# Cross-attention with layer norms: two more vectors loaded as columns, and the softmax's weights left unnormalised up to the last layer norm

## The chip, the cores and the metric

The kernel runs on one core of a Trainium2 chip. A core has a matrix engine (TensorE, PE in the profile, with its weight loads as PEld), a vector engine (VectorE, DVE), a scalar engine (ScalarE, ACT), a general engine (GpSimd, POOL) and a queue that issues transfers (SyncE, SP). Each works through its own list of instructions in order and waits on semaphores for the others. The metric is the time in microseconds on the device, from launch to end. A profile is one execution of the program, with a record for nearly each instruction.

## The reference, cut to what matters

```
text_p  = H_l @ W_text + b_text            # H_l: 4 x 2048 x 512
audio_p = H_a @ W_audio + b_audio          # H_a: 4 x 77 x 384
Q = layer_norm(text_p, g1, beta1);  K = layer_norm(audio_p, g2, beta2);  V = audio_p
alpha = softmax(Q @ K^T / sqrt(512))
H_hyper = (alpha @ V) @ W_out + b_out
out = layer_norm(H_hyper + H_l, g_out, beta_out)
layer_norm(x) = (x - mean) * rsqrt(var + 1e-5) * gamma + beta
```

All is in fp32. The last layer norm is what the change rests on. If a row z is multiplied by a positive number s, its mean and deviation are multiplied by s and its variance by s squared, so that with EPS times s squared in the place of EPS the normalised row is the same. Here s is the sum of the softmax's exponentials of that row.

## The kernel before

**Preparation** (to about 41 us). The keys' input (308 rows, in three blocks) is multiplied by W_audio, normalised (`statistics`, `normed`) and turned (`value_turned`, `key_turned`). W_text is centred and turned into wct (`turn_text`), and its Gram matrix is formed in four parts (`gram`, L633, bank names w_ps). The query is never formed: the score of a row x with a key is x times a matrix of "score weights" m_ps (`score_weights`, L328), 128 x 4 x 80 for each of four blocks of the 512 inputs. Of the 80 columns of each of the four sequences 77 are keys, one is for the bias b_text, and two are padding (S = 77, S1 = 80). They are written zero in kg, on VectorE (L312), and pass through the matmul. `score_offsets` (L346) gives what the biases and beta1 add to the scores, out of rowst, a 128 x 128 stationary operand for each block, whose first 64 columns hold centred b_text times g1, 64 times over, and the last 64 beta1.

To have these as columns, b_text and beta1 are each loaded 64 times over as rows (L158, L159: one tile `rows`, 64 partitions each), b_text is centred on VectorE (L690 to L692), and TensorE turns the tile in four transposes into rows_ps (L698), from which bcv (VectorE, L699) and rowst (ScalarE, L703, L704) are taken. The vectors g1, g2 and beta2 come in another way: as three small loads of 4 x 128 into vec_rows (L152), turned by one transpose (vec_ps, L678) into the columns vec (L679). bc2, the bias's sum of squares, is formed by ScalarE on 64 partitions (L709) and copied to the other 64 (L710).

**The loop** goes over 64 tiles of 128 rows. The tiles are grouped in batches for the small work: twelve of four tiles, then seven of two and two of one. One letter names each step of a tile n or of a batch (named after its first tile):

- p, P: projection of the tile on TensorE (L440 into y, L448 into yl); x: VectorE turns the input of a later tile (L391); t, s: VectorE sums for the norm of the query and adds to the scores (L464, L486)
- r: POOL's rsqrt for the query's norm (L494, L215); c: VectorE scales the scores and takes the maximum (L501, L504); e: ScalarE's exponentials, with their sum by an accumulator (L511)
- w, W: TensorE turns the weights, two tiles at a time (L523), and ScalarE copies them out (L524). The bank is that of yl for the next projection
- i: VectorE takes the reciprocal of the batch's sums, in place (L537)
- a: TensorE multiplies the weights with V @ W_out (L531, bank h); z: VectorE forms z = h * inv + x and its sum (L544)
- q: ScalarE's squares of z less its mean (L552); n: minus the mean (L558); d: variance plus EPS for a batch in one ScalarE instruction (L564), then POOL's rsqrt
- the normalisation is done in one of two ways: o and y on ScalarE (L592, L597) followed by m on POOL (times go, plus beo, L601 and L602), or v and V on VectorE (L581, L583). Each then stores the tile through SP (L571).

The order of the first 40 tiles is a loop over `run`; from then on it is a list written out by hand, for example `p44 v35 o32 r40 i36 y33 W36 V35 z37 a36`. `in_program_order` fixes each engine's list to this order. The planning of buffers (pools of a fixed number of tiles by tag) decides which waits are inserted.

Of the kernel before, what the change touches and what calls it, by code (L numbers as in the profile page):

```python
# [23 lines left out]
F32 = mybir.dt.float32  # L26
# [22 lines left out]
def tile_xattn(  # L49
# [34 lines left out]
    work = ctx.enter_context(tc.tile_pool(name="work", bufs=3))  # L84
    zs = ctx.enter_context(tc.tile_pool(name="zs", bufs=13))
    small = ctx.enter_context(tc.tile_pool(name="small", bufs=8))
    ps1 = ctx.enter_context(tc.tile_pool(name="ps1", bufs=1, space=bass.MemoryType.PSUM))
# [61 lines left out]

    vec_rows = const.tile([3 * NH, P], F32, name="vec_rows")  # L150
    for i, v in enumerate((g1, g2, beta2)):
        nc.sync.dma_start(  # L152
            out=vec_rows[i * NH : (i + 1) * NH, :], in_=v.rearrange("(j p) -> j p", p=P)
        )

    HP = P // 2
    rows = const.tile([P, H], F32, name="rows")
    nc.sync.dma_start(out=rows[:HP], in_=b_text.partition_broadcast(HP))  # L158
    nc.sync.dma_start(out=rows[HP:], in_=beta1.partition_broadcast(HP))  # L159

# [39 lines left out]
    nc.gpsimd.memset(mhalf, -0.5)  # L200
    eps = const.tile([P, 1], F32, name="eps")
    nc.gpsimd.memset(eps, EPS)
    warm = const.tile([P, T], F32, name="warm")
# [14 lines left out]
    rowst = const.tile([P, NH, P], F32, name="rowst")  # L218
    bcv = const.tile([P, NH, 1], F32, name="bcv")
    bc2 = const.tile([P, 1], F32, name="bc2")  # L220
    vec = const.tile([P, 3 * NH], F32, name="vec")
    mu = [const.tile([P, ND, Q, AQ], F32, name=f"mu_{i}") for i in range(2)]
# [87 lines left out]
    def keys_scaled():  # L310

        nc.vector.memset(kg[:, :, :, S:], 0.0)  # L312
        for b in range(B):
            nc.vector.tensor_copy(kg[:, :, b, S : S + 1], bcv)
        for j in range(NH):
            nc.vector.tensor_scalar(
                kg[:, j, :, :S],
                kt[:, j, :].rearrange("p (b s) -> p b s", s=S),
                vec[:, j : j + 1],
                None,  # L320
                ALU.mult,
            )

    def score_weights(k, tag):

        pm = flat(bank(tag, f"m_ps_{k}"))[:, : B * S1].rearrange("p (b s) -> p b s", s=S1)
        for j in range(NH):
            nc.tensor.matmul(  # L328
                pm,
                lhsT=wct[:, j, k * P : (k + 1) * P],  # L330
                rhs=kg[:, j],
                start=(j == 0),
                stop=(j == NH - 1),
            )
        for b in range(2):
            (nc.vector.tensor_copy if b else nc.scalar.copy)(
                mu[b][:, k, :, :SQ], parts(pm[:, b, :])
            )
        nc.scalar.copy(later[:, k], pm[:, 2:, :])
# [68 lines left out]
    class Batch:  # L408


        def __init__(self, tiles):
# [8 lines left out]
            self.ss, self.rs = map(columns, ("ss", "rs"))  # L420
            self.mx, self.inv = map(columns, ("mx", "inv"))
            self.sz, self.sq, self.ro, self.nm = map(columns, ("sz", "sq", "ro", "nm"))
            self.z = {}

# [81 lines left out]
    def exponential(f):  # L506
        s = state[f]
        for q in range(s.m):
            c = slice(q, q + 1)
            e = s.e[:, q, :S]  # L510
            nc.scalar.activation(e, e, AF.Exp, bias=s.mx[:, c], accum_out=s.inv[:, c])  # L511

    def turn_weights(f, a=0):
# [10 lines left out]
        nc.scalar.copy(s.et[:, a:z, :], pe[:S, a:z, :])  # L524

    def apply(n):

        s, c = of(n)
        s.h = getattr(s, "h", {})
        s.h[n] = flat(bank("h", f"h_{n}"))  # L530
        nc.tensor.matmul(  # L531
            s.h[n], lhsT=s.et[:, n - s.tiles[0], :], rhs=s.vw, start=True, stop=True
        )

    def invert(f):
        s = state[f]
        nc.vector.reciprocal(s.inv[:, : s.m], s.inv[:, : s.m])  # L537

    def residual(n):

        i, t = divmod(n, T)
        s, c = of(n)
        z = s.z[n] = zs.tile([P, H], F32, name=f"z_{n}", tag="z")
        nc.vector.scalar_tensor_tensor(  # L544
            z, s.h.pop(n), s.inv[:, c], xs[i][:, t, :], ALU.mult, ALU.add, accum_out=s.sz[:, c]
        )

    def squares(n):
# [11 lines left out]
    def deviations(f):  # L560

        s = state[f]
        m = s.m
        nc.scalar.activation(  # L564
            s.ro[:, :m], s.sq[:, :m], AF.Identity, bias=eps, scale=float(H) ** -3
        )
        rsqrt(s.ro[:, :m], s.ro[:, :m])
# [30 lines left out]

    def norm_on_gpsimd(n):
        z = of(n)[0].z[n]  # L600
        nc.gpsimd.tensor_tensor(z, z, go, ALU.mult)  # L601
        nc.gpsimd.tensor_tensor(z, z, beo, ALU.add)  # L602
        store(n)

# [72 lines left out]
    pt = bank("gain", "vec_ps")  # L677
    nc.tensor.transpose(pt[:, 0, : 3 * NH], vec_rows, ident[: 3 * NH, : 3 * NH])  # L678
    nc.vector.tensor_copy(vec, pt[:, 0, : 3 * NH])  # L679
    value(2, pv[2])  # L680
# [7 lines left out]
    bmean = const.tile([P, 1], F32, name="bmean")  # L688
    b = rows[:HP]
    nc.vector.tensor_reduce(bmean[:HP], b, AX.X, ALU.add)  # L690
    nc.vector.tensor_scalar_mul(bmean[:HP], bmean[:HP], 1.0 / H)
    nc.vector.tensor_scalar(b, b, bmean[:HP], None, ALU.subtract)  # L692
    normed(2)
    gram(1)
    value_turned(2, "prep")
    key_turned(2, "gain")

    pt = rows_turned(rows, P, "h", "rows_ps")  # L698
    nc.vector.tensor_scalar_mul(bcv, pt[:, :, 0:1], 2.0)  # L699
    gram(2)  # L700
    keys_scaled()
    for j in range(NH):
        nc.scalar.mul(rowst[:, j, :HP], pt[:, j, :HP], vec[:, j : j + 1])  # L703
    nc.scalar.mul(rowst[:, :, HP:], pt[:, :, HP:], scale)  # L704
    for k in range(ND - 1):
        gram_out(k)
    gram(3)
    junk = scrap.tile([P, H], F32, name="sqj_b", tag="sqj")
    nc.scalar.activation(junk[:HP], b, AF.Square, accum_out=bc2[:HP])  # L709
    nc.vector.tensor_copy(bc2[HP:], bc2[:HP])  # L710
    gram_out(3)
    turn(0)
    turn(1)
    for k, tag in reversed(list(enumerate(("prep", "h", "gain", "h")))):
        score_weights(k, tag)
    score_offsets()
# [28 lines left out]
    def keep_warm_late(count):  # L745
# [16 lines left out]
        W=lambda f: turn_weights(f, T // 2),  # L762
        i=invert,
        a=apply,
        z=residual,
        q=squares,
        n=minus_mean,
        d=deviations,
        o=norm_shift,
        y=norm_on_scalar,  # L770
        m=norm_on_gpsimd,
        v=lambda n: norm_on_vector(n, 0),
# [12 lines left out]
    for n in range(40):  # L785
# [5 lines left out]
        if t == 0:  # L791
            run([("r", 4)], n)
        run([("v", 12), ("V", 12)] if on_vector else [("m", 12)], n)
        if n == KEPT:
# [13 lines left out]
    for step in """  # L808
        s39 z33
        p40 r36 o28 P40 x42 t40 y30 a35 z35 s40 a34 c36 y31 z34 x43  # L810
        p41 y28 P41 m30 t41 n32 s41
        p42 m31 P42 t42 m28 x44 q34 s42 e36 w36
        p43 q33 x45 q35 P43 t43 a37 d32 s43
        p44 v35 o32 r40 i36 y33 W36 V35 z37 a36 y34 y29 c40 q37 m33 P44 z36 m29 y32 a38 t44 z38 q36 x46 e40
        p45 s44 m34 q38 a39 P45
        p46 P46 z39 t45 n36 q39 s45 t46 d36 x47 x48 w40 i40 s46
        p47 a41 o36 y38 v37 t47 x49 W40 z41 a40 y36 y39 V37 z40 P47 s47 a42 a43
        p48 m32 m38 P48 q41 z42 q40
        p49 q42 r44 x50 z43 q43 t48 n40 c44 m36 d40 s48 v41 e44 w44 P49 a45 t49 o40 x51 V41 m39 y43 a44 W44 i44
        s49 z44 r48 z45  # L820
        p50 t50 y42 q44 a47 x52 c48 q45 z47 P50 e48 a46 q47 m43 s50 z46 v40 m42 q46
        p51 w48 n44 P51 t51 d44 V40
        p52 i48 s51 v47 a49 o44 a48 x54 x53 r50 y46 P52 y45 m46 y44 V47 c50 t52 z48
        p53 e50 z49 q48 w50 q49 P53 s52 m44 a51 t53 n48 d48 a50 s53 i50
        p54 o48 y48 r52 x55 P54 z50 z51 m45 t54
        p55 c52 P55 s54 n50 q51 q50 d50 m48 x57 e52 x56 w52 o50
        p56 t55 x58 s55 P56 y51 v49 r54 i52 t56 V49 a53 x59 c54 a52
        p57 y50 e54 z52 z53 m51 w54 P57 i54 s56 a54 a55 m50 t57
        p58 q53 x60 s57 q52 n52 z55 d52 r56 z54 P58
        p59 o52 t58 y52 c56 q55 s58 v53 e56 i56 q54 w56 P59 n54 a57 m52 d54 t59 o54 V53 y54 y55 s59 a56 z57 r58  # L830
        z56 q56 q57 m54
        p60 c58 x61 t60 P60 x62 n56 d56 e58
        p61 s60 w58 v56 i58 t61 V56 P61 o56 a59 s61 y57 a58
        p62 x63 P62 m55 r60 m57 z59 z58 t62 q59
        p63 n58 c60 q58 d58 s62 v58 t63 e60 r62 w60 i60 V58 c62 o58 P63 s63 a60 e62 w62 r63 z60 i62 y59 a61 q60
        z61 a62 n60 c63 q61 z62 e63 d60 k7 w63 k2 n62 a63 v60 i63 v61 V60 z63 q62 m59 V61 d62 v62 n63 v63 q63 V62 d63
        V63
    """.split():
# [37 lines left out]
```

## Time and profile before

| | us |
|---|---|
| median of 3 runs | 294.62 (294.55 to 294.77) |
| the profiled execution's own time | 294.76 |
| its span, first to last instruction | 293.0 |
| PE busy | 283.7 (97%) |
| DVE busy | 227.1 (78%) |
| ACT busy | 154.5 (53%) |
| POOL busy | 157.6 (54%) |

In the profile a row of a timeline is: start in us, length in us, engine, line, operation, output and inputs with their shapes, how many such instructions were merged, and in brackets how long the engine had been idle before and what ended that. The chain of work that ended last is followed back from the last instruction to what released each step. L numbers are lines of the kernel before. An fp32 matmul has two records in the profile, one for each pass. A row of small DVE instructions may overlap the next, so the distance from start to start is what it takes from the queue.

### The profile page before, as it was taken

What the parts mean: (1) busy time and instruction counts of PE and PEld (TensorE: products, weight loads), DVE (VectorE), ACT (ScalarE), POOL (GpSimd) and SP (SyncE); (2) the same over time, 40 slices, a digit from 0 to 9 for tenths busy, and PEclk for the clock granted to TensorE, in tenths of its full rate; (3) what the DMA queues carried; (4) which work ended last, traced back from release to release, by engine and by line L of the source; (5) the groups of instructions that cost most, each with busy time, mean ns of one, the idle gap of its engine ahead of it and who ended that gap; (6) DMA issues with size and microseconds to landing.
All of it is one profiled execution on the core that took longest, in us unless ns stands there. A gap on an engine that the chain in (4) does not pass through costs nothing.

```text
span 293.0 us, 3988 instructions
## 1 busy us (share of the span) xinstructions
PE 283.7 (97%) x1021; PEld 168.1 (57%) x1021; DVE 227.1 (78%) x713; ACT 154.5 (53%) x490; POOL 157.6 (54%) x168
## 2 busy tenths in 40 slices
PE   7999999999999999999999999999999999999990
PEld 5485755565555555555555565656565555555540
DVE  0784143486878797979797979798999999989996
ACT  3574210041446383737373737357967767477572
POOL 1012000010116667666666676677988978977834
PEclk9999999999999999999999999999999999999996
DMA  7999904358391876878787878789789996712214
GB/s 200 269 306 339 232 12 88 69 175 195 135 242 39 168 261 151 280 160 274 154 277 154 276 159 274 159 272 192 275 172 294 205 258 189 177 72 84 109 62 179
DMA packets 54315, 55.59 MB, mean 190 GB/s; under 512 B 2618, under 2 KB 35706, under 8 KB 54292
## 3 DMA queue, kind: packets, MB, share of 16 engines
q1 hardware_dynamic: 54291, 55.33, 69.9%
q8 instruction: 8, 0.13, 0.2%
q14 instruction: 16, 0.12, 0.1%
HBM read 38.23 MB, written 16.78 MB: 188 GB/s over the span
## 4 chain that ended last, share of the span: by engine, by line
PE 92%; DVE 3%; DMA 2%; issue 1%; SPq 1%; DVEq 0%; ACT 0%
PE y L440 53%; PE h L531 18%; PE yl L448 5%; PE vw_ps L370 4%; PE m_ps L328 3%; PE et_ps L523 2%; PE va_ps L266 2%; PE w_ps_yl L633 2%; DMA wa<-in_L_xattn_W_audio_dram 2%; PE w_ps_y L633 1%; DVE z L583 1%; PE uw_ps L346 1%; DVE z L544 1%; DVE y L581 1%; PE kt_ps L248 0%
## 5 line engine op out<-in xcount | busy, mean ns | idle before, releaser
L440 PE MATMUL y<-mu,xt 128*128 128x464 f32 (+2 forms) x512 | 179.6, 473 | 0.0
L440 PEld LDWEIGHTS y<-mu,xt 128*128 128x128 f32 x512 | 89.7, 190 | 49.6 <-issue 32.3
L531 PE MATMUL h<-vw,et 77*128 77x512 f32 x128 | 64.1, 594 | 0.1
L552 ACT ACTIVATE sqj<-z,sz 128x512 f32<-128x512 f32 x64 | 46.0, 719 | 31.9 <-DVE z L544 30.9
L601 POOL TENSOR_TENSOR z<-z,go 128x512 f32<-128x512 f32 x44 | 56.0, 1272 | 9.9 <-ACT z L597 9.4
L602 POOL TENSOR_TENSOR z<-z,beo 128x512 f32<-128x512 f32 x44 | 55.9, 1271 | 3.4
L544 DVE SCALAR_TENSOR_TENSOR z<-h,inv,x 128x512 f32<-128x512 f32 x64 | 46.4, 732 | 2.3 <-PE h L531 1.7
L391 DVE STREAM_TRANSPOSE xt<-xq 128x512 f32<-128x512 f32 x64 | 44.7, 703 | 0.5 <-PE y L440 0.5
L464 DVE CUSTOM_DVE_ANT_1 yl<-yl,x,bc 128x128 f32<-128x128 f32 x64 | 22.6, 353 | 28.2 <-PE yl L448 28.1
L464 DVE CUSTOM_DVE_ANT_1 y<-y,x,e 128x384 f32<-128x384 f32 x64 | 40.1, 626 | 2.3
L494 POOL TENSOR_SCALAR rs<-ss 128x4 f32<-128x4 f32 (+2 forms) x21 | 4.7, 225 | 67.7 <-DVE ss L464 67.6
L448 PEld LDWEIGHTS yl<-ub,xt 128*128 128x128 f32 x128 | 23.6, 188 | 26.2 <-issue 15.6
L597 ACT ACTIVATE z<-z,no,ro 128x512 f32<-128x512 f32 x44 | 34.5, 802 | 0.1
L524 ACT COPY et<-et_ps 77x256 f32<-77x256 f32 (+1 forms) x33 | 11.9, 362 | 39.4 <-PE et_ps L523 39.4
L215 POOL TENSOR_TENSOR ro<-ro,mhalf 128x4 f32<-128x4 f32 (+2 forms) x21 | 18.2, 869 | 23.8 <-ACT ro L564 23.7
L511 ACT ACTIVATE e<-e,mx 128x77 f32<-128x77 f32 x64 | 22.2, 350 | 11.9 <-DVE mx L504 11.9
L531 PEld LDWEIGHTS h<-vw,et 77*128 77x128 f32 x128 | 23.3, 190 | 7.0 <-issue 5.2
L448 PE MATMUL yl<-ub,xt 128*128 128x128 f32 x128 | 24.5, 273 | 0.0
L215 POOL TENSOR_TENSOR rs<-rs,mhalf 128x4 f32<-128x4 f32 (+2 forms) x21 | 18.6, 887 | 1.7
L486 DVE TENSOR_TENSOR e<-y,uws 128x80 f32<-128x80 f32 x64 | 14.9, 233 | 4.7 <-PE y L440 3.4
L523 PEld LDWEIGHTS et_ps<-ident,e 128*77 128x77 f32 x64 | 9.4, 147 | 15.1 <-issue 10.9
L581 DVE SCALAR_TENSOR_TENSOR y<-z,nm,gain_ps 128x512 f32<-128x512 f32 x20 | 14.9, 751 | 0.8
(112 smaller groups left out, 253.5 us busy)
## 6 DMA issues: line engine op xcount, KB each, us to landing
xq<-in_x_dram SPq DMA_DIRECT2D x64, 256.0 KB, 4.9
x<-in_x_dram SPq DMA_DIRECT2D x16, 1024.0 KB, 6.7
out_dram<-z SPq DMA_DIRECT2D x64, 256.0 KB, 2.3
wc<-in_L_xattn_W_text_dram SPq DMA_DIRECT2D x4, 256.0 KB, 5.7
wo<-in_L_xattn_W_out_dram SPq DMA_DIRECT2D x1, 1024.0 KB
wa<-in_L_xattn_W_audio_dram SPq DMA_DIRECT2D x3, 256.0 KB, 3.6
ba<-in_L_xattn_b_audio_dram SPq DMA_DIRECT2D x1, 256.0 KB, 5.6
bo<-in_L_xattn_b_out_dram SPq DMA_DIRECT2D x1, 256.0 KB
```

The lines of the kernel that those rows point to most:

```text
L215: nc.gpsimd.tensor_tensor(dst, v, mhalf[: v.shape[0], : v.shape[1]], ALU.pow)
L391: nc.vector.transpose(xt.rearrange("p k (a j) -> p a k j", j=R), xq[i][:, t].rearrange("p a (k i) -> p a k i", i=R),)
L440: nc.tensor.matmul(parts(y[:, : Q * AQ])[:, :, cols], lhsT=xt[:, k, :], rhs=mub[:, k, :, cols], start=(k == LAST_K), stop=(k == 0),)
L448: nc.tensor.matmul(b, lhsT=xt[:, k, :], rhs=ub.rearrange("p q i -> p (q i)"), start=True, stop=True)
L464: nc.vector.tensor_tensor_reduce(out=y, in0=y, in1=x, scale=1.0, scalar=first, op0=ALU.mult, op1=ALU.add, accum_out=to)
L511: nc.scalar.activation(e, e, AF.Exp, bias=s.mx[:, c], accum_out=s.inv[:, c])
L531: nc.tensor.matmul(s.h[n], lhsT=s.et[:, n - s.tiles[0], :], rhs=s.vw, start=True, stop=True)
L544: nc.vector.scalar_tensor_tensor(z, s.h.pop(n), s.inv[:, c], xs[i][:, t, :], ALU.mult, ALU.add, accum_out=s.sz[:, c])
L552: nc.scalar.activation(junk, s.z[n], AF.Square, bias=s.sz[:, c], scale=-float(H), accum_out=s.sq[:, c])
L597: nc.scalar.activation(z, z, AF.Identity, bias=s.no[:, c], scale=s.ro[:, c])
L601: nc.gpsimd.tensor_tensor(z, z, go, ALU.mult)
L602: nc.gpsimd.tensor_tensor(z, z, beo, ALU.add)
```

## The change

**b_text and beta1 as columns.** They become two more small loads into vec_rows, which has 20 rows instead of 12, and vec has 20 columns. b_text is still loaded as rows, now on all 128 partitions, for its mean and its sum of squares alone. The centred bias is formed on the columns (bcc, three small VectorE instructions), and rowst is written by two ScalarE instructions that read a column 64 times over. The four transposes of rows are gone, and so is the copy of bc2.

**The padding.** kg's padding is no longer zeroed or multiplied. Instead `score_bank` takes the four banks of m_ps ahead of the matmuls and VectorE writes zero into their padding columns; the matmuls work on 4 x 78 columns.

**No reciprocal.** Step i is now a ScalarE instruction that forms EPS times the square of the sums (ep). Step z forms x times the sum plus h. Step d takes ep as its bias, which is a number for each row and each tile, so that it is one ScalarE instruction for each tile instead of one for each batch. The tile eps on POOL is gone.

**The rest.** The step m is split in two letters, m and M, that always stand side by side. Three new functions, `diagonal`, `apply_sums` and `residual_out` (letters g, b, Z), are defined and no order calls them, so that they issue nothing; the pool diag is unused with them. The order lists are otherwise the same.

```diff
-    vec_rows = const.tile([3 * NH, P], F32, name="vec_rows")
-    for i, v in enumerate((g1, g2, beta2)):
+    vec_rows = const.tile([5 * NH, P], F32, name="vec_rows")
+    for i, v in enumerate((g1, g2, beta2, b_text, beta1)):
...
-    rows = const.tile([P, H], F32, name="rows")
-    nc.sync.dma_start(out=rows[:HP], in_=b_text.partition_broadcast(HP))
-    nc.sync.dma_start(out=rows[HP:], in_=beta1.partition_broadcast(HP))
+    rows = load("rows", [P, H], b_text.partition_broadcast(P))
...
-        nc.vector.memset(kg[:, :, :, S:], 0.0)
         for b in range(B):
-            nc.vector.tensor_copy(kg[:, :, b, S : S + 1], bcv)
+            nc.vector.tensor_copy(kg[:, :, b, S], bcv)
...
+    def score_bank(k, tag):
+        pms[k] = flat(bank(tag, f"m_ps_{k}"))[:, : B * S1].rearrange("p (b s) -> p b s", s=S1)
+        nc.vector.memset(pms[k][:, :, S + 1 :], 0.0)
...
             nc.tensor.matmul(
-                pm,
+                pm[:, :, : S + 1],
                 lhsT=wct[:, j, k * P : (k + 1) * P],
-                rhs=kg[:, j],
+                rhs=kg[:, j, :, : S + 1],
...
-    def invert(f):
+    def sums_squared(f):
+
         s = state[f]
-        nc.vector.reciprocal(s.inv[:, : s.m], s.inv[:, : s.m])
+        nc.scalar.activation(
+            s.ep[:, : s.m], s.sum[:, : s.m], AF.Square, scale=math.sqrt(EPS)
+        )
...
-            z, s.h.pop(n), s.inv[:, c], xs[i][:, t, :], ALU.mult, ALU.add, accum_out=s.sz[:, c]
+            z, xs[i][:, t, :], s.sum[:, c], s.h.pop(n), ALU.mult, ALU.add, accum_out=s.sz[:, c]
...
-        nc.scalar.activation(
-            s.ro[:, :m], s.sq[:, :m], AF.Identity, bias=eps, scale=float(H) ** -3
-        )
+        for q in range(m):
+            c = slice(q, q + 1)
+            nc.scalar.activation(
+                s.ro[:, c], s.sq[:, c], AF.Identity, bias=s.ep[:, c], scale=float(H) ** -3
+            )
...
-    nc.tensor.transpose(pt[:, 0, : 3 * NH], vec_rows, ident[: 3 * NH, : 3 * NH])
-    nc.vector.tensor_copy(vec, pt[:, 0, : 3 * NH])
+    nc.tensor.transpose(pt[:, 0, : 5 * NH], vec_rows, ident[: 5 * NH, : 5 * NH])
+    nc.vector.tensor_copy(vec, pt[:, 0, : 5 * NH])
...
-    b = rows[:HP]
-    nc.vector.tensor_reduce(bmean[:HP], b, AX.X, ALU.add)
-    nc.vector.tensor_scalar_mul(bmean[:HP], bmean[:HP], 1.0 / H)
-    nc.vector.tensor_scalar(b, b, bmean[:HP], None, ALU.subtract)
+    nc.vector.tensor_reduce(bmean, rows, AX.X, ALU.add)
+    nc.vector.tensor_scalar_mul(bmean, bmean, -1.0 / H)
+
+    nc.vector.tensor_scalar(bcc[:, 0], vec[:, 3 * NH : 4 * NH], bmean, None, ALU.add)
+    nc.vector.tensor_tensor(bcc[:, 1], bcc[:, 0], vec[:, :NH], ALU.mult)
+    nc.vector.tensor_scalar_mul(bcv, bcc[:, 0], 2.0)
...
-    pt = rows_turned(rows, P, "h", "rows_ps")
-    nc.vector.tensor_scalar_mul(bcv, pt[:, :, 0:1], 2.0)
     gram(2)
     keys_scaled()
-    for j in range(NH):
-        nc.scalar.mul(rowst[:, j, :HP], pt[:, j, :HP], vec[:, j : j + 1])
-    nc.scalar.mul(rowst[:, :, HP:], pt[:, :, HP:], scale)
+
+    nc.scalar.copy(rowst[:, :, :HP], bcc[:, 1].unsqueeze(2).to_broadcast([P, NH, HP]))
+    nc.scalar.mul(
+        rowst[:, :, HP:], vec[:, 4 * NH :].unsqueeze(2).to_broadcast([P, NH, HP]), scale
+    )
+    for k, tag in enumerate(("prep", "h", "gain", "h")):
+        score_bank(k, tag)
...
-    nc.scalar.activation(junk[:HP], b, AF.Square, accum_out=bc2[:HP])
-    nc.vector.tensor_copy(bc2[HP:], bc2[:HP])
+    nc.scalar.activation(junk, rows, AF.Square, bias=bmean, accum_out=bc2)
```

More of the change, by code (lines that the diff above doesn't have):

```diff
@@ L85, in tile_xattn @@
     zs = ctx.enter_context(tc.tile_pool(name="zs", bufs=13))
+    diag = ctx.enter_context(tc.tile_pool(name="diag", bufs=3))
     small = ctx.enter_context(tc.tile_pool(name="small", bufs=8))
@@ L200, in tile_xattn @@
     nc.gpsimd.memset(mhalf, -0.5)
-    eps = const.tile([P, 1], F32, name="eps")
-    nc.gpsimd.memset(eps, EPS)
     warm = const.tile([P, T], F32, name="warm")
@@ L218, in tile_xattn @@
     rowst = const.tile([P, NH, P], F32, name="rowst")
-    bcv = const.tile([P, NH, 1], F32, name="bcv")
+    bcv = const.tile([P, NH], F32, name="bcv")
     bc2 = const.tile([P, 1], F32, name="bc2")
-    vec = const.tile([P, 3 * NH], F32, name="vec")
+    vec = const.tile([P, 5 * NH], F32, name="vec")
+    bcc = const.tile([P, 2, NH], F32, name="bcc")
     mu = [const.tile([P, ND, Q, AQ], F32, name=f"mu_{i}") for i in range(2)]
@@ L322, in keys_scaled, with score_weights @@
             )
-    def score_weights(k, tag):
-        pm = flat(bank(tag, f"m_ps_{k}"))[:, : B * S1].rearrange("p (b s) -> p b s", s=S1)
+    pms = {}
+    def score_bank(k, tag):
+        pms[k] = flat(bank(tag, f"m_ps_{k}"))[:, : B * S1].rearrange("p (b s) -> p b s", s=S1)
+        nc.vector.memset(pms[k][:, :, S + 1 :], 0.0)
+    def score_weights(k):
+        pm = pms[k]
         for j in range(NH):
             nc.tensor.matmul(
-                pm,
+                pm[:, :, : S + 1],
                 lhsT=wct[:, j, k * P : (k + 1) * P],
-                rhs=kg[:, j],
+                rhs=kg[:, j, :, : S + 1],
                 start=(j == 0),
@@ L420, in __init__ @@
             self.ss, self.rs = map(columns, ("ss", "rs"))
-            self.mx, self.inv = map(columns, ("mx", "inv"))
+            self.mx, self.sum, self.ep = map(columns, ("mx", "sum", "ep"))
             self.sz, self.sq, self.ro, self.nm = map(columns, ("sz", "sq", "ro", "nm"))
-            self.z = {}
+            self.z, self.h = {}, {}
     def of(n):
@@ L510, in exponential @@
             e = s.e[:, q, :S]
-            nc.scalar.activation(e, e, AF.Exp, bias=s.mx[:, c], accum_out=s.inv[:, c])
+            nc.scalar.activation(e, e, AF.Exp, bias=s.mx[:, c], accum_out=s.sum[:, c])
     def turn_weights(f, a=0):
@@ L524, in turn_weights, with diagonal, apply_sums @@
         nc.scalar.copy(s.et[:, a:z, :], pe[:S, a:z, :])
+    def diagonal(n):
+        s, c = of(n)
+        s.dg = getattr(s, "dg", {})
+        s.dg[n] = diag.tile([P, P], F32, name=f"dg_{n}", tag="dg")
+        nc.scalar.mul(s.dg[n], ident, s.sum[:, c])
+    def apply_sums(n):
+        i, t = divmod(n, T)
+        s, c = of(n)
+        s.h[n] = flat(bank("h", f"h_{n}"))
+        nc.tensor.matmul(s.h[n], lhsT=s.dg.pop(n), rhs=xs[i][:, t, :], start=True, stop=False)
     def apply(n):
         s, c = of(n)
-        s.h = getattr(s, "h", {})
-        s.h[n] = flat(bank("h", f"h_{n}"))
+        first = n not in s.h
+        if first:
+            s.h[n] = flat(bank("h", f"h_{n}"))
         nc.tensor.matmul(
-            s.h[n], lhsT=s.et[:, n - s.tiles[0], :], rhs=s.vw, start=True, stop=True
+            s.h[n], lhsT=s.et[:, n - s.tiles[0], :], rhs=s.vw, start=first, stop=True
         )
-    def invert(f):
+    def sums_squared(f):
         s = state[f]
-        nc.vector.reciprocal(s.inv[:, : s.m], s.inv[:, : s.m])
+        nc.scalar.activation(
+            s.ep[:, : s.m], s.sum[:, : s.m], AF.Square, scale=math.sqrt(EPS)
+        )
     def residual(n):
@@ L544, in residual, with residual_out @@
         nc.vector.scalar_tensor_tensor(
-            z, s.h.pop(n), s.inv[:, c], xs[i][:, t, :], ALU.mult, ALU.add, accum_out=s.sz[:, c]
+            z, xs[i][:, t, :], s.sum[:, c], s.h.pop(n), ALU.mult, ALU.add, accum_out=s.sz[:, c]
         )
+    def residual_out(n):
+        s, c = of(n)
+        z = s.z[n] = zs.tile([P, H], F32, name=f"z_{n}", tag="z")
+        nc.scalar.activation(z, s.h.pop(n), AF.Identity, accum_out=s.sz[:, c])
     def squares(n):
@@ L597, in norm_on_scalar, with norm_on_gpsimd @@
         nc.scalar.activation(z, z, AF.Identity, bias=s.no[:, c], scale=s.ro[:, c])
-    def norm_on_gpsimd(n):
+    def norm_on_gpsimd(n, step):
         z = of(n)[0].z[n]
-        nc.gpsimd.tensor_tensor(z, z, go, ALU.mult)
-        nc.gpsimd.tensor_tensor(z, z, beo, ALU.add)
-        store(n)
+        nc.gpsimd.tensor_tensor(z, z, beo if step else go, ALU.add if step else ALU.mult)
+        if step:
+            store(n)
     nmean = const.tile([P, ND], F32, name="nmean")
@@ L713, in tile_xattn @@
     turn(1)
-    for k, tag in reversed(list(enumerate(("prep", "h", "gain", "h")))):
-        score_weights(k, tag)
+    for k in reversed(range(ND)):
+        score_weights(k)
     score_offsets()
@@ L762, in tile_xattn @@
         W=lambda f: turn_weights(f, T // 2),
-        i=invert,
+        i=sums_squared,
         a=apply,
+        b=apply_sums,
+        g=diagonal,
         z=residual,
+        Z=residual_out,
         q=squares,
@@ L770, in tile_xattn @@
         y=norm_on_scalar,
-        m=norm_on_gpsimd,
+        m=lambda n: norm_on_gpsimd(n, 0),
+        M=lambda n: norm_on_gpsimd(n, 1),
         v=lambda n: norm_on_vector(n, 0),
@@ L792, in tile_xattn @@
             run([("r", 4)], n)
-        run([("v", 12), ("V", 12)] if on_vector else [("m", 12)], n)
+        run([("v", 12), ("V", 12)] if on_vector else [("m", 12), ("M", 12)], n)
         if n == KEPT:
@@ L810, in tile_xattn @@
         p40 r36 o28 P40 x42 t40 y30 a35 z35 s40 a34 c36 y31 z34 x43
-        p41 y28 P41 m30 t41 n32 s41
-        p42 m31 P42 t42 m28 x44 q34 s42 e36 w36
+        p41 y28 P41 m30 M30 t41 n32 s41
+        p42 m31 M31 P42 t42 m28 M28 x44 q34 s42 e36 w36
         p43 q33 x45 q35 P43 t43 a37 d32 s43
-        p44 v35 o32 r40 i36 y33 W36 V35 z37 a36 y34 y29 c40 q37 m33 P44 z36 m29 y32 a38 t44 z38 q36 x46 e40
-        p45 s44 m34 q38 a39 P45
+        p44 v35 o32 r40 i36 y33 W36 V35 z37 a36 y34 y29 c40 q37 m33 M33 P44 z36 m29 M29 y32 a38 t44 z38 q36 x46
@@ L816, in tile_xattn @@
+        e40
+        p45 s44 m34 M34 q38 a39 P45
         p46 P46 z39 t45 n36 q39 s45 t46 d36 x47 x48 w40 i40 s46
         p47 a41 o36 y38 v37 t47 x49 W40 z41 a40 y36 y39 V37 z40 P47 s47 a42 a43
[L818 to L821, printed above, removed]
+        p48 m32 M32 m38 M38 P48 q41 z42 q40
@@ L822, in tile_xattn @@
+        p49 q42 r44 x50 z43 q43 t48 n40 c44 m36 M36 d40 s48 v41 e44 w44 P49 a45 t49 o40 x51 V41 m39 M39 y43 a44
+        W44 i44 s49 z44 r48 z45
+        p50 t50 y42 q44 a47 x52 c48 q45 z47 P50 e48 a46 q47 m43 M43 s50 z46 v40 m42 M42 q46
         p51 w48 n44 P51 t51 d44 V40
[L823 to L826, printed above, removed]
+        p52 i48 s51 v47 a49 o44 a48 x54 x53 r50 y46 P52 y45 m46 M46 y44 V47 c50 t52 z48
@@ L827, in tile_xattn @@
+        p53 e50 z49 q48 w50 q49 P53 s52 m44 M44 a51 t53 n48 d48 a50 s53 i50
+        p54 o48 y48 r52 x55 P54 z50 z51 m45 M45 t54
+        p55 c52 P55 s54 n50 q51 q50 d50 m48 M48 x57 e52 x56 w52 o50
         p56 t55 x58 s55 P56 y51 v49 r54 i52 t56 V49 a53 x59 c54 a52
-        p57 y50 e54 z52 z53 m51 w54 P57 i54 s56 a54 a55 m50 t57
+        p57 y50 e54 z52 z53 m51 M51 w54 P57 i54 s56 a54 a55 m50 M50 t57
         p58 q53 x60 s57 q52 n52 z55 d52 r56 z54 P58
-        p59 o52 t58 y52 c56 q55 s58 v53 e56 i56 q54 w56 P59 n54 a57 m52 d54 t59 o54 V53 y54 y55 s59 a56 z57 r58
@@ L831, in tile_xattn @@
-        z56 q56 q57 m54
+        p59 o52 t58 y52 c56 q55 s58 v53 e56 i56 q54 w56 P59 n54 a57 m52 M52 d54 t59 o54 V53 y54 y55 s59 a56 z57
+        r58 z56 q56 q57 m54 M54
         p60 c58 x61 t60 P60 x62 n56 d56 e58
         p61 s60 w58 v56 i58 t61 V56 P61 o56 a59 s61 y57 a58
-        p62 x63 P62 m55 r60 m57 z59 z58 t62 q59
+        p62 x63 P62 m55 M55 r60 m57 M57 z59 z58 t62 q59
         p63 n58 c60 q58 d58 s62 v58 t63 e60 r62 w60 i60 V58 c62 o58 P63 s63 a60 e62 w62 r63 z60 i62 y59 a61 q60
-        z61 a62 n60 c63 q61 z62 e63 d60 k7 w63 k2 n62 a63 v60 i63 v61 V60 z63 q62 m59 V61 d62 v62 n63 v63 q63 V62 d63
@@ L837, in tile_xattn @@
-        V63
+        z61 a62 n60 c63 q61 z62 e63 d60 k7 w63 k2 n62 a63 v60 i63 v61 V60 z63 q62 m59 M59 V61 d62 v62 n63 v63 q63 V62
+        d63 V63
     """.split():
```

## The prediction

> **What bounds the kernel now.** I read the busy shares first, then the chain that ended last, then that chain in order of time for the preparation and for the end, and last the queues of VectorE (DVE), ScalarE (ACT) and GpSimd (POOL) around the changed lines. The profiled execution took 294.76 us with a span of 293.0, so 1.76 us lie outside the span; the median of the runs is 294.62. I sum against the profiled execution and carry the difference over to the median.
>
> ```profile
> PE 283.7 (97%) x1021; PEld 168.1 (57%) x1021; DVE 227.1 (78%) x713; ACT 154.5 (53%) x490; POOL 157.6 (54%) x168
> PE 92%; DVE 3%; DMA 2%; issue 1%; SPq 1%; DVEq 0%; ACT 0%
> ```
>
> The chain is TensorE almost throughout. A table by stage (columns: busy time of PE, PEld, DVE, ACT, POOL, granted clock, DMA share, GB/s) shows where that is strict:
>
> ```profile
> 21.30:37.00 15.70, 15.70 (x56) 10.01 (x55) 5.16 (x21) 6.05 (x23) 1.71 (x4) 1.00 1.03 284
> 41.00:188.00 147.00, 147.00 (x515) 85.52 (x513) 114.62 (x369) 68.56 (x224) 72.61 (x70) 1.00 0.69 181
> 188.00:277.00 89.00, 89.00 (x314) 52.63 (x313) 81.77 (x258) 60.49 (x190) 73.83 (x74) 1.00 0.72 194
> 277.00:293.00 16.00, 8.39 (x31) 4.01 (x30) 12.59 (x33) 7.34 (x28) 6.76 (x11) 0.85 0.31 115
> ```
>
> From 21.3 to 277 us TensorE has no gap at full granted clock. So work taken off TensorE there is gained in full, work added elsewhere is free until TensorE has to wait for it, and the last 16 us are a latency chain of their own. The chain in the preparation (start, length, what):
>
> ```profile
> 20.41 0.35 PE vat_ps L248 x4
> 20.77 0.57 PE kt_ps L248 x4
> 21.34 0.44 PE rows_ps L248 x4
> 21.78 6.02 PE w_ps_yl L633 x16
> 27.80 8.61 PE m_ps L328 x32
> 36.41 2.08 PE uw_ps L346 x8
> ```
>
> **The preparation, TensorE.** The four transposes of rows_ps go: 0.44 us. Before them the chain holds kt_ps, after them gram products that read only wct, finished long before, so these move up. The 16 score-weight matmuls (32 records, two passes each) shrink from 320 to 312 columns. 8.61 / (16 x 320) = 1.68 ns per column, so 16 x 8 x 1.68 = 0.215 us go. That the columns now come as four pieces of 78 costs nothing by the nearest row: the six y records after yl (three matmuls of two passes, one 464 wide, one in four pieces of 84, one in four of 52) take 1.70 us for 464 + 336 + 208 = 1008 columns, also 1.69 ns each. vec_ps turns 20 rows instead of 12: 8 more columns at the transposes' 0.44 / 512 = 0.86 ns, +0.007. Sum -0.65.
>
> **Does something else now arrive late there?** vec_ps waits for five small loads instead of three. SP issues them from 7.7 us, two more at the 0.27 to 0.29 us of the vec_rows rows, and one broadcast of 256 KB (like ba, 0.43) instead of two of 128 KB (0.575 and 0.551). So xq, wo and x behind them are issued 0.1 us earlier, not later. The b_text load issued at 9.06 landed in 3.8, so the small loads issued just before are in by about 13; vec_ps starts at 15.88. Cover 2.9 us. In the VectorE queue:
>
> ```profile
> 19.60 0.14 DVE L691 TENSOR_SCALAR bmean<-bmean 64x1 f32<-64x1 f32 x1
> 19.78 0.48 DVE L692 TENSOR_SCALAR rows<-rows,bmean 64x512 f32<-64x512 f32 x1
> 20.18 0.53 DVE L291 TENSOR_SCALAR kn<-va,kmv,kr 103x512 f32<-103x512 f32 x1
> 20.77 0.38 PEld L248 LDWEIGHTS kt_ps<-ident,kn 103*128 103x128 f32 x4 [0.20 <-DVE kn L291]
> ```
>
> TensorE does wait here, for kn. L692 (0.40 from its start to kn's) is replaced by three operations on 4 columns, each starting 0.08 (kg copies: 0.39 for four) to 0.18 us (bmean to L692, which reads its result) after the last: 0.34 to 0.44. I take 0.34 to 0.40: kn is 0 to 0.06 earlier; bounds -0.06 and +0.14 if all three cost 0.18. Value 0.
>
> The four memsets of the score banks are new and stand ahead of all four score-weight products. The row is the kg memset, 0.10. The Trainium skill (Perfetto Trace Analysis, Optimizing Scalar/DVE Operations) puts a VectorE access to PSUM at about 125 ns against 60 in SBUF, which speaks against this move: 0.40 us by the row, 4 x 0.165 = 0.66 by the rule, an estimate. Either way kg is complete near 23.2 (the last kt leaves ACT at 22.8), the memsets end before 24 and the first score-weight product is due at 27.80 - 0.65 = 27.15. Cover 3 us; gram_out's copies behind them have the same. I take the rule's value, and it changes nothing. rowst becomes two ACT operations instead of five, bc2 loses a copy, L709 works on 128 rows at the same 0.62: all in covers of over 2 us. The eps memset on POOL (0.10) had no one waiting.
>
> **The loop.** Per batch VectorE loses a reciprocal (L537, 21 of 0.13 to 0.17 us, 0.08 to 0.15 from start to start); ACT gains one small square (nearest row L558, 0.195, next start 0.11 to 0.13 later) and, for each tile after the first, one bias-and-scale operation on 128x1. Nearest: L592, four in 0.84 us, so 0.185 each from start to start. That is 0.56 per batch of four and 0.19 per batch of two: 12 x 0.56 + 7 x 0.19 + 21 x 0.12 = 10.6 us more on ACT, which is 53% busy. Moving `i` is what the skill advises against (ScalarE: Activation LUTs, Rules for kernel authors: simple arithmetic goes to VectorE). By that rule alone the square loses 21 x 0.04 us against the reciprocal; by the rows it leaves an engine 92% busy (81.77 of 89.0) for one at 68% in the stretch where it could matter. On the path both are 0.
>
> Whether ACT's lateness reaches TensorE is read from its queue (idle before, in brackets):
>
> ```profile
> 99.46 0.30 ACT L564 ACTIVATE ro<-sq,eps 128x4 f32<-128x4 f32 x1
> 102.67 0.72 ACT L552 ACTIVATE sqj<-z,sz 128x512 f32<-128x512 f32 x1 [2.91 <-DVE z L544]
> 106.43 0.36 ACT L511 ACTIVATE e<-e,mx 128x77 f32<-128x77 f32 x1 [0.59 <-DVE mx L504]
> 109.25 0.37 ACT L524 COPY et<-et_ps 77x256 f32<-77x256 f32 x1 [0.63 <-PE et_ps L523]
> ```
>
> The 0.56 + 0.12 fall into the 2.91 us. In the hand-ordered part the tightest places are batch 32/36 at 202 to 206 us (ACT late by 0.68 against 0.61 idle: the copy et of W36 starts 0.07 late, read over 1 us later by the h product at 207.14) and batch 56 at 261 (POOL's rsqrt, rs behind it and the VectorE scaling of scores behind that, some 0.15 late against a VectorE wait of 0.23 just after). TensorE sees neither. On POOL the rsqrt starts up to 0.56 later per batch, and the go and beo products and their stores behind it; they recover in idle of 1.1 to 2.9 us. The split of L601/L602 into two steps leaves POOL's order as it was. Loop: 0.
>
> **The end.** VectorE loses the reciprocals of batches 60 and 63 on the chain (about 0.08 each); that of 62 stood before a wait for h. ACT gains a square before L597 (+0.11) and one ro operation in batch 60 (+0.19).
>
> ```profile
> 284.37 0.70 POOL L215 TENSOR_TENSOR ro<-ro,mhalf 128x2 f32<-128x2 f32 x1 [2.23 <-ACT ro L564]
> 284.54 0.15 DVE L537 RECIPROCAL inv<-inv 128x1 f32<-128x1 f32 x1
> 284.62 0.73 DVE L581 SCALAR_TENSOR_TENSOR y<-z,nm,gain_ps 128x512 f32<-128x512 f32 x1
> 284.85 1.12 PE L531 MATMUL h<-vw,et 77*128 77x512 f32 x2
> 285.26 0.74 DVE L583 SCALAR_TENSOR_TENSOR z<-y,ro,beo 128x512 f32<-128x512 f32 x1
> 286.01 0.75 DVE L544 SCALAR_TENSOR_TENSOR z<-h,inv,x 128x512 f32<-128x512 f32 x1
> ```
>
> ACT comes 0.08 early from batch 60, so with the square it is 0.03 late, then with its own second ro 0.16 later at POOL: rsqrt ends 285.23 instead of 285.07. L583 of tile 60 can then start near 285.3 instead of 285.26, although VectorE is free at 285.10; z63 waits for h (ends 285.97) as before. So the two savings are eaten by the late ro: 0 to -0.08 if the h product comes early, +0.10 if the signal from POOL is slow. Value -0.03. Every change is 0.65 + 0.03 = 0.68 us; 294.62 - 0.68 = 293.94, or 292.3 of span.
>
> **The rivals.** (1) The gain is partly given back: kn at +0.14 and the end at +0.10, or a TensorE stall of a few tenths that the overlapped weight loads hide today. For it: PEld of yl waits for ACT's et copy 22 times. Against: that copy follows idle ACT time. 294.3.
> (2) The end gains more: without reciprocals and with h early, 0.08 to 0.16 per batch for 60 and 63, and kn 0.06 earlier. 293.5 to 293.6. Against: the late ro.
> (3) Slower: the z operation on VectorE, 64 times, now reads x first and the PSUM bank second. The skill (Vector Engine (DVE) Microarchitecture Reference, Points that are easy to get wrong) says that this operation halves its rate with two sources in SBUF that are not bf16; here one is in PSUM before and after, and L581, which reads PSUM second, takes 751 ns against 732. I take +0.02, inside the cover. Were it halved, another 512 columns at 1.07 ns (L464: 626 ns for 384 columns, 353 for 128) would add 0.55: in 188 to 277 us 28 of them cost 15.4 us against 7.2 idle and 1.5 of dropped reciprocals, so 6.7 us of stall, and three on the end's chain 1.6: about 302.2. It decides from about +0.32 each, where 28 and 3 of them pass those 8.7 us by the forecast's gain and 0.59.
> (4) The change doesn't reach the end because VectorE paces the loop: 294.6. Against: VectorE waited 28.1 us for yl of TensorE.
>
> **How the numbers follow.** Main case 0.66 (293.6 to 294.15), rival 2 0.10, rival 1 with 4 0.14, rival 3 and an ACT stall of that sort 0.10. A measurement of this kernel can tell about 0.2%, 0.59 us, and the forecast of 0.68 is just beyond: of the main case I count 0.60 as faster and 0.06 as same. Faster 0.70, same 0.20, slower 0.10. Leaving out the slow rival and the outer edges of the others, the range is 293.4 to 294.5.
>
> **What would show it.** No rows_ps; m_ps at 8.39 us in the chain; the first y product about 0.65 earlier (37.83 for 38.48); PE without gaps until about 276.3; ro four times 0.185 apart; the last L583 some 0.7 earlier. Wrong would be a z above 0.78, a PE wait for et or e before 276, or L583 of tile 60 waiting for ro by over 0.2.

## The result

The changed kernel is slower by a little: 295.27 us median (294.50 to 295.78) against 294.61 of the kernel before in the same comparison, a ratio of 1.0020 (95% interval 1.0013 to 1.0026). The forecast was 293.94, so it misses by 1.3 us and has the sign wrong. The profiled execution took 295.47 us with a span of 293.7 (before: 294.76 and 293.0); what lies outside the span is the same 1.8.

### The profile after: the work came out as forecast

The busy shares, the chain's shares and one row of the costliest groups, from the page after:

```profile
PE 283.5 (97%) x1017; PEld 168.0 (57%) x1017; DVE 225.0 (77%) x695; ACT 163.1 (56%) x551; POOL 157.4 (54%) x167
PE 94%; DMA 1%; ACT 1%; issue 1%; SPq 0%; DVEq 0%; DVE 0%
L565 DVE SCALAR_TENSOR_TENSOR z<-x,sum,h 128x512 f32<-128x512 f32 x64 | 45.8, 723 | 2.6 <-PE h L549 1.4
```

VectorE has 18 instructions fewer, ScalarE 61 more, and z with the PSUM bank as its second source takes 723 ns for 732 before. The chain in the preparation (start, length, what):

```profile
20.88 0.57 PE kt_ps L246 x4
21.45 6.04 PE w_ps_yl L662 x16
27.49 8.40 PE m_ps L331 x32
35.89 2.07 PE uw_ps L349 x8
37.96 0.78 PE y L443 x2
```

rows_ps is gone, and m_ps takes 8.40 us for 8.61. From the start of kt_ps to the first y product it is 37.96 - 20.88 = 17.08 us, for 38.48 - 20.77 = 17.71 before: 0.63 less. (kt_ps itself starts 0.11 later here; over all kernels below it starts anywhere from 20.32 to 21.27, with the first loads.) The table by stage, columns as in the prediction:

```profile
188.00:277.00 89.00, 89.00 (x313) 52.50 (x312) 81.13 (x249) 64.51 (x219) 74.21 (x75) 1.00 0.72 193
277.00:294.00 17.00, 7.87 (x30) 3.81 (x28) 11.98 (x29) 7.42 (x30) 6.24 (x10) 0.84 0.29 108
```

TensorE is still without a gap up to 277 at full clock. The end, in order of time:

```profile
283.50 0.47 ACT L593 ACTIVATE ro<-sq,ep 128x1 f32<-128x1 f32 x2
284.04 0.70 POOL L212 TENSOR_TENSOR ro<-ro,mhalf 128x2 f32<-128x2 f32 x1 [2.48 <-ACT ro L593]
284.77 0.75 DVE L612 SCALAR_TENSOR_TENSOR z<-y,ro,beo 128x512 f32<-128x512 f32 x1
285.49 0.75 DVE L565 SCALAR_TENSOR_TENSOR z<-x,sum,h 128x512 f32<-128x512 f32 x1
288.14 1.40 DVE L612 SCALAR_TENSOR_TENSOR z<-y,ro,beo 128x512 f32<-128x512 f32 x2
```

and the row of before that answers to the last:

```profile
288.67 1.40 DVE L583 SCALAR_TENSOR_TENSOR z<-y,ro,beo 128x512 f32<-128x512 f32 x2
```

The last two normalisations start 0.53 us earlier than before. Up to here the change does what the forecast says. Yet the span is 0.7 longer.

### Where the time went: behind the last instruction

Exact to the nanosecond in the trace, VectorE's last normalisation ends at 289.543 and the span at 293.687: 4.14 us, against 292.979 - 290.066 = 2.91 before. So 1.23 us are lost after all arithmetic is done. SP's wait for the last stores to land (us in total, times, longest), before:

```profile
SPq L871 <- DMA out_dram<-z: 1.5, 2, 0.9
```

and after:

```profile
SPq L907 <- DMA out_dram<-z: 2.7, 1, 2.7
```

The transfers from 290 to 293 us (packets, MB, share of 16 engines), after:

```profile
q1 hardware_dynamic: 244, 0.43, 39.6%
q14 instruction: 1, 0.01, 0.6%
```

In the same stretch the kernel before has no line for q14:

```profile
q1 hardware_dynamic: 289, 0.52, 47.0%
```

That one packet is a fetch of 8 KB of instructions. It starts at 291.447, amid the store of the last tile, and takes 309 ns. The store has 16 parts. In the trace's record of landings 15 of them are in by 291.630; the 16th lands at 292.802. Its closing 4-byte write, which the other parts began by 291.265, begins at 291.753, as the fetch ends (291.447 + 0.309 = 291.756). Before, the corresponding fetch lay at 284.589 and all 16 parts landed by 292.134, the last 0.03 us after the 15th. From the last landing to the end of the span it is 0.85 us before and 0.89 after.

### The profile page after: what moved, and what is told of

Read it like the earlier page. It is cut to its first block, busy times and chain, and to the rows that moved or that the text cites. A ratio compares the mean times of both kernels' runs of the same rounds, so it can differ in the third digit from the quotient of the medians.

```text
span 293.7 us, 4026 instructions
## 1 busy us (share of the span) xinstructions
PE 283.5 (97%) x1017; PEld 168.0 (57%) x1017; DVE 225.0 (77%) x695; ACT 163.1 (56%) x551; POOL 157.4 (54%) x167
## 4 chain that ended last, share of the span: by engine, by line
PE 94%; DMA 1%; ACT 1%; issue 1%; SPq 0%; DVEq 0%; DVE 0%
PE y L443 54%; PE h L549 18%; PE yl L451 5%; PE vw_ps L373 4%; PE m_ps L331 3%; PE et_ps L526 3%; PE va_ps L264 2%; PE w_ps_yl L662 2%; DMA wa<-in_L_xattn_W_audio_dram 1%; PE w_ps_y L662 1%; PE uw_ps L349 1%; PE kt_ps L246 0%; ACT sqj L579 0%; PE vat_ps L246 0%; DVEq L907 0%
## 5 line engine op out<-in xcount | busy, mean ns | idle before, releaser
L565 DVE SCALAR_TENSOR_TENSOR z<-x,sum,h 128x512 f32<-128x512 f32 x64 | 45.8, 723 | 2.6 <-PE h L549 1.4
L621 ACT ACTIVATE no<-nm,ro 128x1 f32<-128x1 f32 x60 | 13.0, 282 | 4.7 <-POOL ro L212 4.7
```

The lines of the kernel that those rows point to most:

```text
L565: nc.vector.scalar_tensor_tensor(z, xs[i][:, t, :], s.sum[:, c], s.h.pop(n), ALU.mult, ALU.add, accum_out=s.sz[:, c])
```

## The experiments

**Theory 1**: it is a fetch of VectorE's instructions. VectorE's list became shorter, so the fetch that its list asks for at a fixed place moved from 284.6 us into the last store. **Theory 2**: the end of SP's queue, or a load that the change alters, delays the close. A version of theory 1 to be told apart: the fetch is another engine's.

The changed kernel's 295.27 stands beside 294.61 of the kernel before; the others were measured beside it in three groups, in which its median was 294.66, 294.67 and 294.69. So medians of different rows compare through their ratios. The table shows for each kernel the length of VectorE's list against that of before (the busy count), the median, the ratio with its interval, and from its profiled execution: the start of the last fetch; how many of VectorE's records (waits and branches included) had begun by then; how much later than the 15th the 16th part of the last store landed; and the time from the end of VectorE's last normalisation to the end of the span.

```
kernel                          list  median  ratio (95% interval)      fetch    begun  16th late  tail
before                             0  294.61  -                         284.589   831     0.03     2.91
changed kernel                   -18  295.27  1.0020 (1.0013, 1.0026)   291.447   831     1.17     4.14
 + 16 VectorE memsets             -2  294.14  0.9978 (0.9971, 0.9986)   283.853   830     0.04     2.91
 + 6 VectorE memsets             -12  294.22  0.9985 (0.9978, 0.9992)   287.740   833     0.15     3.07
 + 2 VectorE memsets             -16  294.44  0.9992 (0.9985, 0.9999)   289.109   833     0.43     3.34
 + 16 GpSimd memsets             -18  294.86  1.0001 (0.9992, 1.0010)   290.842   831     1.18     4.09
 8 VectorE instructions fewer    -26  294.35  0.9984 (0.9977, 0.9990)   294.666   828     0.04     2.97
before, no reciprocal only       -21  294.70  1.0006 (0.9997, 1.0014)   293.770   831     0.03     2.92
 the same + 3 VectorE memsets    -18  295.14  1.0013 (1.0006, 1.0020)   292.322   831     0.44     3.37
columns and padding only          +3  294.03  0.9977 (0.9970, 0.9984)   283.519   833     0.04     2.92
changed kernel, again            -18  295.06  1.0013 (1.0004, 1.0022)   291.652   831     1.17     4.14
 + 16 GpSimd memsets, again      -18  295.03  1.0011 (1.0003, 1.0019)   291.306   831     0.47     3.38
 + 16 VectorE memsets, again      -2  294.20  0.9982 (0.9973, 0.9991)   283.359   830     0.03     2.92
```

### VectorE's list made longer again

```diff
+    pad = const.tile([P, 1], F32, name="pad")
+    for _ in range(16):
+        nc.vector.memset(pad, 0.0)
     gram(3)
```

The memsets stand in the preparation, where VectorE has cover. Two more kernels have 6 and 2 of them. Sixteen:

> The changed kernel with 16 one-column VectorE memsets of a tile that nobody reads, in the preparation where VectorE is idle. Theory 1 (a block of VectorE's instructions, 8 KB on queue 14, is fetched just when the last store is under way, because VectorE's list became 18 instructions shorter): the fetch falls back to where it lay before, 6 to 8 us before the end, the last store lands about 2.1 us after it is issued, and the kernel takes 294.0 to 294.3, faster than the kernel before by 0.3 to 0.6. Theory 2 (the last store is late because SP issues one transfer more, which shifts the stores among queues and semaphores): nothing moves, 295.2 to 295.4.

294.14: work that does nothing makes the kernel 1.1 us faster (0.86 where both ran in one group, below). The fetch is at 283.853 again and the tail at 2.91. Its last normalisations start within 0.05 us of those of the changed kernel, and SP's wait is back at 1.5:

```profile
288.19 1.41 DVE L612 SCALAR_TENSOR_TENSOR z<-y,ro,beo 128x512 f32<-128x512 f32 x2
...
SPq L910 <- DMA out_dram<-z: 1.5, 1, 1.5
```

Six:

> As the run with 16 memsets, with 6. Theory 1: the fetch comes 6 VectorE instructions earlier, about 4 us, so between 286 and 288 us; it may then meet an earlier store, whose lateness nobody waits for: 294.0 to 294.4. Theory 2: 295.2 to 295.4.

294.22, the fetch at 287.740. Two:

> The changed kernel with 2 VectorE memsets. By 16, 6 and 0 memsets (fetch at 283.9, 287.7 and 291.4 us) the fetch should start between 289 and 291 us, in the stores of the last two tiles. If it takes its toll only from a store that it falls into, and the last one alone counts, between 294.1 and 295.3.

294.44, the fetch at 289.109, and a part of the loss is there (0.43 late). With 16, 6, 2 and 0 memsets the fetch is at 283.9, 287.7, 289.1 and 291.4. Theory 2 doesn't fit any of these, since SP's queue and the loads are those of the changed kernel.

### The change in halves

The one half alone: the kernel before with the square in the place of the reciprocal, z in its new form and ro tile by tile.

```diff
-        nc.vector.reciprocal(s.inv[:, : s.m], s.inv[:, : s.m])
+        nc.scalar.activation(s.ep[:, : s.m], s.inv[:, : s.m], AF.Square, scale=math.sqrt(EPS))
...
-            z, s.h.pop(n), s.inv[:, c], xs[i][:, t, :], ...
+            z, xs[i][:, t, :], s.inv[:, c], s.h.pop(n), ...
```

> The kernel before with the reciprocal's removal alone (21 VectorE instructions fewer, ep and ro on ScalarE), b_text and beta1 as before. Theory 1: VectorE's list is 3 shorter than that of the changed kernel, so the fetch either stays in the last store (295.0 to 296.0, slower than before by 0.4 to 1.4) or is not made at all (294.5 to 294.7). Theory 2: no transfer was added, so the end is as before: 294.5 to 294.7, with the fetch wherever it is.

294.70, no different from before, which both theories allow. Its list is three instructions shorter even than that of the changed kernel, and the fetch is made all the same, at 293.770, 1.1 us behind the end of the span (292.669), so that no store is late. It still doesn't seem to be free. What lies between a run's time and its span is 1.93 us on average here, for 1.78 of the kernel before in the same group and 1.78 to 1.79 in every kernel whose last fetch is made within the span; the kernel with 8 instructions fewer, the other one with the fetch behind the end, has 2.00. That the late fetch is the reason is likely, but was not tested. From the first y product to the last normalisations it takes 288.35 - 38.17 = 250.18 us, for 288.67 - 38.48 = 250.19 before: this half brings 0.01 on the path.

The other half: the changed kernel with the reciprocal, z and ro of before.

> The changed kernel with the reciprocal and the common ro of before: the columns and the padding alone. VectorE's list is 3 instructions longer than in the kernel before. Theory 1: the fetch lies early, TensorE's 0.65 us come out at the end: 293.9 to 294.2. Theory 2: SP has its extra transfer, so the last store is late: 295.0 to 295.4.

294.03, the fastest of all. The preparation is 17.08 as in the changed kernel, VectorE's list three longer than before, and the fetch at 283.519. SP's loads are those of the changed kernel, so theory 2 falls here again.

### The loss made in a kernel that didn't have it

Three idle memsets put into the first half bring VectorE's list to the length of the changed kernel's (713 - 21 + 3 = 695):

> The kernel without the reciprocal alone, with three one-column VectorE memsets that nobody reads, in the preparation. VectorE's list is then as long as in the changed kernel, and SP's as in the kernel before. If the fetch in the last store is set by the length of VectorE's list alone, three idle instructions of 0.1 us bring it back: the fetch starts near 291.5 to 292, one of 16 parts of the last store lands about 1 us late, 295.2 to 295.8. If something else of the full change is needed, 294.6 to 294.8.

295.14 for 294.70, through three instructions of no use and no place on the path (its preparation is 17.72, its loop 250.18). The two kernels ran in different groups, and the intervals of their ratios overlap. Their spans alone, without what the one without memsets pays behind the end, are 293.35 and 292.86 us on average, for 292.96 and 292.93 of the kernel before beside them, and the tail in the profiles is 3.37 for 2.92. The fetch is at 292.322, in its last store:

```profile
q1 hardware_dynamic: 385, 0.69, 53.6%
q14 instruction: 1, 0.01, 0.6%
```

(transfers from 290 to 293.5 us). The median falls just short of what was expected, and the 16th part is 0.44 late, not 1.17.

### VectorE's list made shorter still

```diff
-        for b in range(B):
-            nc.vector.tensor_copy(kg[:, :, b, S], bcv)
+        nc.vector.tensor_copy(kg[:, :, :, S], bcv.unsqueeze(2).to_broadcast([P, NH, B]))
...
-        nc.vector.memset(pms[k][:, :, S + 1 :], 0.0)
+        nc.scalar.copy(pms[k][:, :, S + 1 :], zeros[:, :8].rearrange("p (b s) -> p b s", s=2))
...
-        nc.vector.memset(uws[:, :, 0, S:], 0.0)
+        nc.gpsimd.memset(uws[:, :, 0, S:], 0.0)
```

> The changed kernel with 8 VectorE instructions fewer: the bias column is written by one copy instead of four, ScalarE zeroes the padding of the four banks, POOL the padding of uws. If the length of VectorE's list decides, the fetch falls behind the last landing, as in the run without the reciprocal alone: 294.0 to 294.3. If any shorter VectorE list is bad, 295.2 or more.

294.35, just above what was expected. The fetch has moved past the end (294.666, span to 292.899), the tail is 2.97, preparation and loop take 17.08 and 250.18. Taking instructions away cures the late store as adding them does. Without the 0.22 us more that this kernel has outside its span (2.00 for 1.78) it would stand at 294.13.

### Whose fetch it is

```diff
+    for _ in range(16):
+        nc.gpsimd.memset(pad, 0.0)
     gram(3)
```

> The changed kernel with 16 one-column memsets on POOL instead of VectorE, in the preparation, where POOL is idle too. If the fetch is of VectorE's instructions, it stays in the last store: 295.1 to 295.5, and the fetch near 291.4. If it is POOL's, or if any instruction added before the end helps, 294.0 to 294.3.

294.86, between the two expectations. The trace is plain, though: the fetch stays in the last store (290.842) and the 16th part is 1.18 late. To see whether GpSimd's memsets bring something of their own, this kernel, the changed one and the one with 16 VectorE memsets were put beside each other once more:

> The changed kernel once more, beside the next two on one chip. If the fetch of VectorE's instructions at the end of the last store is the whole loss: 295.1 to 295.5, and 1.0 to 1.2 us above the kernel with 16 VectorE memsets.

> The 16 GpSimd memsets once more. If the 294.86 of their first run against the 295.27 of the changed kernel was a difference between chips: within 0.2 us of the changed kernel in this comparison. If GpSimd's padding itself brings something: 0.3 to 0.5 us below it. In both cases the last landing is over 0.4 us later than the 15 others of its store.

> The 16 VectorE memsets once more, beside the changed kernel: 294.0 to 294.3, no fetch in the last store, its last landing within 0.05 us of the one before.

295.06, 295.03 and 294.20. The changed kernel comes out a little under its expectation, 0.86 us above the kernel with VectorE's memsets where 1.0 to 1.2 were expected, and the GpSimd memsets bring nothing that can be told from zero. Why their first run gave 294.86 stays open: the intervals of the two runs of this kernel (0.9992 to 1.0010 and 1.0003 to 1.0019) overlap. SP waits 2.7 us for the last landing in the changed kernel again, and 1.5 in the one with VectorE's memsets.

That the fetch is VectorE's rests on four things. First, memsets added on VectorE alone move it, and 16 added on GpSimd don't. Second, what the GpSimd memsets do move is another fetch, which lies at 274.83 and 274.77 us in the two profiles of the changed kernel and at 260.63 and 261.11 with them. Third, in the eleven profiles where the last fetch comes before the end, VectorE has begun 830 to 833 of its records, while GpSimd has begun anything from 199 to 222 and ScalarE from 532 to 607; in the two others VectorE's whole list has 828 and 831 records, and the fetch comes after the end. (In the five profiles with VectorE's list at -18, and in the one at -16, the last record counted is the last normalisation, behind which VectorE only waits for the end, so that there the count alone doesn't fix the time.) TensorE's count is nearly as constant, 1084 to 1091, but the VectorE memsets leave its list as it is, and in the changed kernel its last matmul ends at 285.46. Fourth, in the five profiles at -18 the fetch follows the end of VectorE's last normalisation by 1.85 to 1.91 us, though that end itself lies between 288.99 and 290.41.

## Why the prediction was wrong

Step by step:

- **The preparation, TensorE, -0.65**: right. 0.44 for rows_ps, 8.61 - 8.40 = 0.21 for m_ps, +0.02 for the gram products: 0.63. Every kernel with the columns has 17.08 us from kt_ps to the first y, every one without them 17.71 or 17.72.
- **kn, value 0**: right. From L721 (19.87) to kn (20.28) it is 0.41 us in place of L692's 0.40; kt_ps starts within the scatter of the loads in both kinds of kernel.
- **The memsets of the score banks**: hidden, as said. The Trainium skill's access cost (Perfetto Trace Analysis, Optimizing Scalar/DVE Operations), from which the prediction estimated 0.66 us for the four, was too high here: their rows are 0.065 us each, and from the start of the copy before them (23.33) to the next row of VectorE (23.72) it is 0.39 us for the copy and all four.
- **The loop, 0**: right. From the first y to the last normalisations it is 250.18 us for 250.19. The four ro take 0.84 us, 0.28 for one, so (0.84 - 0.28) / 3 = 0.187 apart, for 0.185 expected. ScalarE's busy time grew by 8.6, not 10.6. No wait of PE for et or e is new before 276.
- **The end, -0.03**: right as to VectorE (-0.01 with the loop), and for the reason given. L612 of tile 60 starts at 284.77, 0.76 us after the L610 before it, where rows that wait for nothing follow each other at 0.66. It waits some 0.1 us for ro, which GpSimd finishes at 284.74, and loses nothing by it, since z of tile 63 waits for its h until 285.46.
- **Rival 3**, a slower z with PSUM second: refuted, 723 ns for 732. Rivals 1, 2 and 4 did not occur either.
- **The step that failed** is the sum: "Every change is 0.65 + 0.03 = 0.68 us; 294.62 - 0.68". It carries over, uncounted, what lies behind VectorE's last instruction: 2.91 us of store, landing and close. They became 4.14, +1.23, because a fetch of VectorE's instructions fell into the last store. Less the 0.53 by which the last normalisations came earlier, that is the +0.7 of the span. No case of the forecast held it: each step was asked what engine it moves work to, and none what the count of instructions does. Taking away the 21 reciprocals, counted as 0 on the path, is what moved the fetch: without that half VectorE's list grows by three.

With the collision taken away the sum holds: -0.52 us by medians with 16 memsets (-0.49 the second time) and -0.63 with the columns alone, all with intervals that take in 0.63.

Shown is that the place of the fetch decides: it was moved out both ways, and into a kernel that hadn't had it. It costs 1.17 or 1.18 us in three profiles and 0.44 and 0.47 in two others, and the trace shows what tells them apart. In all five the data of the 16th part end 0.18 to 0.19 us behind those of the other parts. In the three costlier ones the fetch then comes ahead of the 16th part's 4-byte write, which begins only as the fetch ends, 0.49 us after the last of the others, and lands 1.05 us later. In the two others (the first half with 3 memsets, and the second run of the GpSimd memsets) the write begins 6 ns ahead of the fetch, 0.18 after the others, and lands 0.61 and 0.65 later. In the kernel before it is 0.36 from the write to the landing. Why a landing next to a fetch takes longer is not explained, nor what decides which of the two goes first. The medians of the colliding kernels (295.27, 295.06, 295.03, 295.14, 294.86) may hold both prices. Nor was it tried to keep the fetch in place and move the store.

## What to carry to other kernels

Ask of a change what it does to the number of instructions on each engine, the idle ones too: here the fetches of an engine's list ran on the transfer engines that carry the stores, and the one that fell into the last store delayed the end by more than its own length. In a profile this is a q14 packet between the last arithmetic and the end, with SP's wait for the last landing grown and one part of the store late; look there first when all work ends earlier and the span doesn't. A fetch behind the end is in no store's way, but compare the time outside the span too: it was 0.16 and 0.22 us longer in the two kernels that had one. Here a change worth 0.6 us lost 1.2 by it, and 6 to 16 empty instructions (or using only the half that pays) bring the gain home: 294.03 to 294.22 us for some 294.7.

## What was not expected of the hardware

An instruction fetch of 309 ns delayed the last part of a 256 KB store by 0.44 to 1.18 us. The place of the last fetch was the same in VectorE's list within three records wherever it could be told, so that counting could foretell about where a change would put it. A fetch 1.4 us before the end of VectorE's last normalisation (287.740, with 6 memsets) and one right at it (289.109, with 2) still went with a 16th part that was 0.15 and 0.43 us late, although the last tile's store was at most just being issued.
